# Moving a token tile's preparation steps in the v stage of an attention kernel

## The chip, the cores and the metric

The kernel runs on one core of one Trainium2 chip. The metric is device time in microseconds (us) of one launch, median over several runs. All numbers are float32; the large matrix products are made from operands that are split into a high part and a low part, with three passes (high x high, high x low, low x high).

## The reference, cut to what matters

The reference normalises `x` (4 x 512 tokens of 512 features), runs a lightning attention with 16 heads of width 128 over it, and multiplies its output with a gate from a router (softmax over 64 experts, top 8). The part that this case is about is the first one, the normalised tokens and the product that gives `v`:

```python
xn = _layernorm(x, axis=-1)                                   # x: 4 x 512 x 512
qkv = silu(einsum('bnf,of->bno', xn, w_qkv))                   # v is a third of it
...
logits = einsum('th,eh->te', xn, router_weight) + router_bias  # from the same tokens
```

The attention proper, the norm over all heads, the output product and the gate follow. They are not touched.

## The kernel before, in words

TensorE makes nearly every product, and each of the other engines works through its own list in the order in which the program issues it. No scheduler reorders anything: the order is written out by hand. VectorE (DVE in the profile) does the adds out of PSUM and part of the splits, ScalarE (ACT) the copies, the casts to the high part and the SiLU, GpSimd (POOL) most of the low parts, SyncE (SP) the transfers.

**Token tiles.** The 2048 tokens are handled as eight tiles `(p, t)`: `p` is a pair of sequences (two of four), `t` a block of 128 tokens in each. A tile is prepared in these steps (`prepare`, line 849): `stats` (BN statistics on VectorE, and a power on GpSimd that gives `rstd`), `norms` (two normalisations on VectorE), `turn` (eight transposes on TensorE, two copies by ScalarE into `xf`), `sums` (four subtractions of 128x256 into `ts`, which give T1 to T4), `plain` (high and low parts of B11, B21 and B22) and `more` (high and low parts of T1 to T4). A high part is a cast on ScalarE (line 100), a low part a subtraction (line 103) on the engine named.

**Units of v.** The loop at line 957 runs over sixteen units `k`: unit `k` multiplies one tile with one of two groups of v's weights, the first eight units with group 0. Units 0 and 1 use plain block products (`plain_unit`, line 554), the others a Strassen form with seven products (`unit`, line 515), 6 matmuls each. In a Strassen unit three PSUM banks are used several times:

- product one writes bank 0, and ScalarE copies it to `s1`; product four accumulates onto bank 0, so it waits for that copy;
- product two writes bank 1, and VectorE adds `a` = bank 1 + `s1`; product five starts bank 1 again and waits for `a`;
- product three writes bank 2, and VectorE adds `e` = bank 2 + `a`; product six accumulates onto bank 2 and waits for `e`;
- after product five VectorE adds bank 1 and `e` into the output `vo11`; product seven accumulates onto bank 1 and waits for that add. The outputs `vo01` and `vo10` come after products six and seven.

**The list `after`.** While unit `k` runs, the steps of later tiles are issued between its products. `after[i]` holds what is issued behind product i + 1; `after[0]` is behind product one. The transposes of tile k + 1 stand behind product one. The engines' queues follow that order: an instruction that stands in front of an add on VectorE delays it. The weights need the same treatment: `sum_of` (line 452) makes four weight sums on VectorE, 128x1024 each, behind product four in units 3 to 6 for group 1; `split_one` (line 475) splits a weight block. `split_rw` (line 310) splits the router's weights once, in time for `logits` in unit 8.

**Outputs.** `vout` is the pool for the outputs of a unit, 128x512 each (`sink`, line 598), and for three temporaries of `logits`. A place in it is free again when its store has landed.

The functions that the change touches and what calls them:

Of the kernel before, what the change touches and what calls it, by code (L numbers as in the profile page):

```python
# [50 lines left out]
def kernel(  # L51
# [13 lines left out]
    nc = tc.nc  # L65
# [5 lines left out]
    NT = N // P  # L71
# [6 lines left out]
    def pool(stack, name, bufs=1, **kw):  # L78
        return stack.enter_context(tc.tile_pool(name=name, bufs=bufs, **kw))


    def left(stack, name, bufs=1):
        return pool(stack, name, bufs, side="left", reuse_waits="tile")
# [15 lines left out]
    def split_hi(hi, src):  # L99
        nc.scalar.copy(hi, src)  # L100

    def split_lo(eng, lo, src, hi):
        eng.tensor_tensor(lo, src, hi.bitcast(F32), ALU.subtract)  # L103
# [74 lines left out]
    stats = [const.tile([P, NT, 2], F32, tag=f"stats{b}", name=f"stats{b}") for b in range(B)]  # L178
# [59 lines left out]
    def normalise_x(p, t):  # L238
        for b in range(p * PB, p * PB + PB):
            normalise(xts[b, t], xts[b, t], b, t)  # L240

    xfs = {}


    def transpose(stage, p, j, t, copy=True):
        b = p * PB + j
        if j == 0:
            xfs[p, t] = stage.tile([P, PB, FC, P], F32, tag="xf", name=f"xf_{p}_{t}", bufs=2)
        pt = ps_sc.tile([P, FC, P], F32, tag="sc", name=f"pt_{b}_{t}")
        for c in range(FC):  # L250
            nc.tensor.transpose(pt[:, c, :], xts[b, t][:, bass.ts(c, P)], ident)  # L251
        if copy:
            nc.scalar.copy(xfs[p, t][:, j], pt)
        return pt

    def halves(xf):
        return xf[:, 0, 0:KC], xf[:, 1, 0:KC], xf[:, 0, KC:], xf[:, 1, KC:]

    def split_blocks(p, t, eng, srcs):
        for n, src in srcs:  # L260
            blk = blocks[p, n][:, t]
            split_hi(blk[:, 0], src)
            split_lo(eng, blk[:, 1], src, blk[:, 0])


    def token_sums(eng, xf, s):
        b11, b12, b21, b22 = halves(xf)
        sub = lambda d, a, b: lambda: eng.tensor_tensor(d, a, b, ALU.subtract)
        subs = [
            sub(s[:, 0], b12, b11), sub(s[:, 1], b22, s[:, 0]),  # L270
            sub(s[:, 2], b22, b12), sub(s[:, 3], b21, s[:, 1]),
        ]
        return subs, {
            "B11": b11, "B21": b21, "B22": b22, "T1": s[:, 0], "T2": s[:, 1], "T3": s[:, 2], "T4": s[:, 3],
        }


    def combine(stage, p, t, eng, again=""):
        src = {}

        def sums():
            s = stage.tile([P, 4, KC, P], F32, tag="ts", name=f"ts_{p}_{t}{again}", bufs=1)
            subs, of = token_sums(eng, xfs[p, t], s)
            src.update(of)
            for f in subs:
                f()

        def split(which):
            split_blocks(p, t, eng, [(n, src[n]) for n in XN if n[0] == which])
        return sums, lambda: split("B"), lambda: split("T")  # L290


    def plain(p, t, eng):
        b11, b12, b21, b22 = halves(xfs[p, t])
        split_blocks(p, t, eng, (("B11", b11), ("T1", b12), ("B21", b21), ("B22", b22)))
# [14 lines left out]
    def split_rw(stage):  # L310
        rwr.append(stage.tile([P, FC, 2, E], F32R, tag="rwr", name="rwr", bufs=1))
        split_hi(rwr[0][:, :, 0], rw)
        split_lo(nc.vector, rwr[0][:, :, 1], rw, rwr[0][:, :, 0])
# [533 lines left out]
    NP_FIRST = 2  # L847

    def prepare(stage, p, t):
        first = (p, t) == (0, 0)  # L850

        def turn():
            for j in range(PB):
                transpose(stage, p, j, t)
            if p == 0:
                nc.sync.dma_start(out=xf_d[t], in_=xfs[p, t])

        if p == 0 and t < NP_FIRST:
            sums = (lambda: plain(p, t, nc.vector if t == 0 else nc.gpsimd)), lambda: None, lambda: None
        else:  # L860
            sums = combine(stage, p, t, nc.gpsimd)

        return {
            "stats": lambda: layer_norms(p, t, first), "norms": lambda: normalise_x(p, t),
            "turn": turn, "sums": sums[0], "plain": sums[1], "more": sums[2],
        }
# [33 lines left out]
    vw_stack, vs_stack = ExitStack(), ExitStack()  # L900
    stage = right(vs_stack, "stage", 4)
    rawp, sump = right(vs_stack, "vraw"), right(vs_stack, "vsum")
    vwp, vout = left(vw_stack, "vw", 8), left(vw_stack, "vout", 4)
    ws = [v_weights(0, g, rawp, sump, vwp) for g in range(NV)]
    tiles = [(p, t) for p in range(NP) for t in range(NT)]
    again = [(p, t) for p in reversed(range(NP)) for t in range(NT)]
    n1 = len(tiles)
    prep = [prepare(stage, p, t) for p, t in tiles]

    load_pair(stage, 0, 0)  # L910
# [46 lines left out]
    for k, (p, t) in enumerate(tiles + again):  # L957
        g, after = k // n1, nothing()
        if n1 - NT <= k < n1:
            after[6].append(lambda p=p, t=t: keep_blocks(p, t))  # L960
        if k + 1 < n1:
            after[0 if k else 1].append(prep[k + 1]["turn"])
            if 0 < k < n1 - 3:
                after[0].append(lambda k=k: load_pair(stage, *tiles[k + 3]))
            if k == 0:
                after[1].insert(0, prep[2]["stats"])
            after[1].append(prep[k + 1]["sums"])
            if k + 2 < n1:
                if k:
                    after[1].append(prep[k + 2]["stats"])  # L970
                after[4 if k > 1 else 3].append(prep[k + 2]["norms"])
            after[1].append(prep[k + 1]["plain"])
            after[4].append(prep[k + 1]["more"])
        if k == 0:
            after[0].append(lambda: warm_up(8, xfs[0, 0][:, 1, 0]))
        if k == n1 - 1:
            after[2].append(lambda: split_rw(stage))
        for unit_of, p2 in ((n1, 1), (n1 + NT + 1, 0)):
            if k == unit_of:
                less = [lambda p2=p2, what=what: scores_less(p2, what) for what in ("top", "less")]  # L980
                for j, f in enumerate(logits(stage, p2, vout) + less):
                    after[j].append(f)
        if k < NP_FIRST:
            for i in range(2):
                n, eng = f"S{2 * k + i + 1}", nc.gpsimd if i else nc.vector
                after[2 * i + 2].append(lambda i=2 * k + i: ws[0].sum_of(i, nc.vector))
                after[2 * i + 3].append(lambda n=n, eng=eng: ws[0].split_one(n, eng))
        if k == NP_FIRST:
            after[0].append(ws[1].load())
        if n1 - 5 <= k < n1 - 1:  # L990
            after[3].append(lambda n=k - n1 + 5: ws[1].sum_of(n, nc.vector))
        for n, unit_of, step, eng, piece in (
            ("A11", n1 - 2, 6, nc.gpsimd, None), ("S2", n1 - 1, 0, nc.gpsimd, None),
            ("S1", n1 - 1, 1, nc.gpsimd, None), ("A12", n1 - 1, 2, nc.vector, 0),
            ("S3", n1 - 1, 3, nc.gpsimd, None), ("A12", n1 - 1, 4, nc.vector, 1),
            ("S4", n1, 1, nc.vector, 0), ("S4", n1, 2, nc.vector, 1), ("A22", n1, 0, nc.gpsimd, None),
        ):
            if k == unit_of:
                after[step].append(lambda n=n, eng=eng, piece=piece: ws[1].split_one(n, eng, piece))
        if n1 <= k < n1 + NT:  # L1000
            after[0].append(lambda t=t: load_xf(stage, t))
        if n1 < k <= n1 + NT:
            sums, split_plain, split_sums = combine(stage, 0, k - n1 - 1, nc.gpsimd, "r")
            after[1] += [sums, split_plain]
            after[4].append(split_sums)
        if k == NP_FIRST:
            after[0].append(keep_rows)
        if k >= n1:
            for i in range(2):
                after[3 * i + 2].append(lambda h=2 * (k - n1) + i: keep_decay(h))  # L1010
        if k == n1 + NT + 2:
            after[0].append(scores_exp)
        if k == 2 * n1 - 2:
            vs_stack.close()
            todo = [(p, *u) for p in range(NP) for u in h_units(p, hw_stack)]
            todo[0][3].load()()
            todo[1][3].load()()
        if k == 2 * n1 - 1:
            weight_steps(todo[0][3], after)
        v_unit(p, g, t, ws[g], vout, after, k < NP_FIRST)  # L1020
# [29 lines left out]
    again = right(rb_stack, "again")  # L1050
# [5 lines left out]
    for i, (p, kind, n, w) in enumerate(todo):  # L1056
        after = nothing()
# [161 lines left out]
```

## Time and profile before

| | us |
|---|---|
| median of 3 runs | 1064.3 |
| lowest and highest | 1062.9, 1064.8 |
| profiled execution, its own time | 1063.0 |
| span of the profiled execution | 1061.2 |
| TensorE busy in it | 1050.7 |
| VectorE, ScalarE, GpSimd busy | 524.3, 521.8, 663.7 |

TensorE's clock was granted in full (0.999). The first 189 us of the span are the v stage; units 0 to 7, in which the tiles are prepared, lie between 11 and 103 us. From 40 to 100 us GpSimd is busy 57.5 of 60 us and VectorE 41.5. A line of the timeline gives start, duration, engine, line, operation, output and inputs, shapes and count, and in brackets the idle time of the engine before it and what ended it. A line of waits gives who waited for whom, the total, how often, and the longest.

### The profile page before, as it was taken

To read this page: it belongs to the slowest core of one execution; us is meant where nothing else is said; L and a number is where in the kernel's file an instruction comes from. 1 tells how busy PE (TensorE), PEld (TensorE's weight loads), DVE (VectorE), ACT (ScalarE), POOL (GpSimd) and SP (SyncE) were. 2 spreads that over 40 slices of the span, in tenths; PEclk is the share of its full clock that TensorE was granted. 3 is DMA by queue.
4 is the path that set the end of the run, shared out by engine and by line. 5 is a ranking of instruction groups with operands and counts; after the bars stand their busy time and mean duration, and the time that the engine had idled before them with its cause. 6 is when DMAs were issued, how large, how long until landed. Compare 5 with 4: busy or idle time off the path is not lost.

```text
span 1061.2 us, 16043 instructions
## 1 busy us (share of the span) xinstructions
PE 1050.7 (99%) x5707; PEld 906.1 (85%) x5707; DVE 524.3 (49%) x872; ACT 521.8 (49%) x960; POOL 663.7 (63%) x694
## 2 busy tenths in 40 slices
PE   9899999999999999999999999999999999999998
PEld 7687888888888888888888888888888888888886
DVE  6676434355454545444444444444444456745354
ACT  5556454655555555455555555554555543332221
POOL 5899571757777678677785777767867756402020
PEclk9999999999999999999999999999999999999999
DMA  7467655422423223334822242232322446455351
GB/s 243 163 231 285 225 172 171 154 86 85 140 85 95 78 94 117 96 124 156 290 91 65 85 129 86 85 102 90 107 66 85 157 132 217 136 162 171 99 189 50
DMA packets 109871, 143.07 MB, mean 135 GB/s; under 512 B 9680, under 2 KB 58208, under 8 KB 108896
## 3 DMA queue, kind: packets, MB, share of 16 engines
q1 hardware_dynamic: 108752, 141.35, 41.3%
q8 instruction: 45, 0.74, 0.3%
q10 hardware_dynamic: 1040, 0.71, 0.2%
q14 instruction: 34, 0.28, 0.1%
HBM read 93.24 MB, written 50.87 MB: 136 GB/s over the span
## 4 chain that ended last, share of the span: by engine, by line
PE 95%; DVE 0%; issue 0%
PE u_qk L533 29%; PE po L838 16%; PE u_g L533 14%; PE u_v L533 12%; PE o L726 5%; PE sa L689 5%; PE o L728 4%; PE ss L712 4%; PE kt L692 2%; PE pu L783 1%; PE lg L324 1%; PE pt L251 0%; PE ssq L755 0%; PE lt L350 0%; PE pw L419 0%
## 5 line engine op out<-in xcount | busy, mean ns | idle before, releaser
L838 PE MATMUL po<-wr,yr 128*128 128x512 f32 (+1 forms) x777 | 178.7, 388 | 0.9 <-DVE u L825 0.9
L838 PEld LDWEIGHTS po<-wr,yr 128*128 128x128 f32 x777 | 144.4, 188 | 30.4 <-DVE u L825 1.1
L533 PE MATMUL u_qk<-blk_T,ws_qk 128*128 128x512 f32 x576 | 147.0, 395 | 0.0
L738 POOL TENSOR_TENSOR sqs<-sqs,sq 128x512 f32<-128x512 f32 x60 | 77.9, 1298 | 76.3 <-ACT sq L737 76.3
L533 PEld LDWEIGHTS u_qk<-blk_T,ws_qk 128*128 128x128 f32 x576 | 105.8, 188 | 20.2
L103 POOL TENSOR_TENSOR ws_qk<-sum_qk,ws_qk 128x512 fp32r<-128x512 f32 x64 | 82.8, 1294 | 40.5 <-ACT ws_qk L100 39.6
L533 PE MATMUL u_qk<-blk_B,wa_qk 128*128 128x512 f32 x384 | 99.1, 394 | 0.0
L726 PE MATMUL o<-at,vin 128*128 128x128 f32 x512 | 88.5, 275 | 0.0
L533 PEld LDWEIGHTS u_qk<-blk_B,wa_qk 128*128 128x128 f32 x384 | 71.0, 188 | 14.1
L103 DVE TENSOR_TENSOR yr<-yin,yr 128x512 fp32r<-128x512 f32 x64 | 60.6, 960 | 43.0 <-ACT yr L100 42.1
L103 POOL TENSOR_TENSOR ws_g<-sum_g,ws_g 128x512 fp32r<-128x512 f32 x32 | 41.3, 1289 | 59.9 <-ACT ws_g L100 59.9
L726 PEld LDWEIGHTS o<-at,vin 128*128 128x128 f32 x512 | 74.9, 192 | 2.5
L533 PE MATMUL u_g<-blk_T,ws_g 128*128 128x512 f32 x288 | 76.0, 400 | 0.0
L698 ACT ACTIVATE kd<-kt,kdecay 128x384 f32<-128x384 f32 x64 | 37.2, 582 | 78.0 <-PE kt L692 78.0
L730 DVE SCALAR_TENSOR_TENSOR y<-o,nw,gt 128x512 f32<-128x512 f32 x64 | 48.1, 751 | 55.1 <-PE o L728 55.1
L728 PE MATMUL o<-qd,st 128*128 128x128 f32 x384 | 74.3, 275 | 0.0
L737 ACT ACTIVATE sq<-o 128x512 f32<-128x512 f32 x60 | 35.9, 598 | 75.2 <-POOL sqs L738 42.4
L716 DVE SCALAR_TENSOR_TENSOR st<-st,bdecay,ss 128x128 f32<-128x128 f32 x128 | 41.7, 346 | 58.9 <-ACT st L714 56.6
L826 POOL TENSOR_TENSOR u<-u,x 128x512 f32<-128x512 f32 x12 | 17.8, 1515 | 84.0 <-DVE u L825 84.0
L100 ACT CAST yr<-yin 128x512 fp32r<-128x512 f32 x64 | 39.2, 616 | 63.2 <-PE po L838 39.2
L577 ACT ACTIVATE k<-k 128x512 f32<-128x512 f32 x64 | 40.4, 632 | 57.1 <-DVE k L524 57.1
L689 PE MATMUL sa<-q,k 128*128 128x128 f32 x512 | 67.5, 275 | 0.0
(192 smaller groups left out, 2296.1 us busy)
## 6 DMA issues: line engine op xcount, KB each, us to landing
v<-vo_v SPq DMA_DIRECT2D x64, 256.0 KB, 2.2
raw_qk<-in_w_head_dram SPq DMA_DIRECT2D x64, 256.0 KB, 3.8
vin<-v SPq DMA_DIRECT2D x64, 256.0 KB, 3.6
y<-y SPq DMA_DIRECT2D x64, 256.0 KB, 2.0
yin<-y SPq DMA_DIRECT2D x64, 256.0 KB, 2.8
x<-in_x_dram SPq DMA_DIRECT2D x32, 256.0 KB, 4.6
raw_g<-in_w_head_dram SPq DMA_DIRECT2D x32, 256.0 KB, 3.0
raw_v<-in_w_v_dram SPq DMA_DIRECT2D x16, 256.0 KB, 6.1
```

The costliest lines, as they stand in the source:

```text
L100: nc.scalar.copy(hi, src)
L103: eng.tensor_tensor(lo, src, hi.bitcast(F32), ALU.subtract)
L533: nc.tensor.matmul(ps, lhsT, rhs, start=(first and c == 0 and n == 0), stop=(c == KC - 1 and n == len(PASSES) - 1), skip_group_check=not f ...
L577: nc.scalar.activation(dst, src, AF.Silu)
L689: nc.tensor.matmul(pa[:, c], k[:, c], q[:, c], start=True, stop=True)
L712: nc.tensor.matmul(ps[:, c], kd[s][:, c], v_of(b, h, c), start=True, stop=True)
L716: nc.vector.scalar_tensor_tensor(r[:, c], r[:, c - 1], bdecay[:, h : h + 1], ps[:, c], ALU.mult, ALU.add)
L726: nc.tensor.matmul(o, v_of(b, h, c), at[s][:, c], start=True, stop=(c == 0))
L728: nc.tensor.matmul(o, st[s][:, c - 1], qd[s][:, c - 1], start=False, stop=True)
L730: nc.vector.scalar_tensor_tensor(y, po, nw[:, h : h + 1], gts[s], ALU.mult, ALU.mult)
L738: nc.gpsimd.tensor_tensor(sq[b], sq[b], s1, ALU.add)
L838: nc.tensor.matmul(pos[t][:, c], yr[:, yi, bass.ts(t, P)], wos[h][:, wi, c], start=(h == 0 and n == 0), stop=(h in stops and n == len(PASS ...
```

## The change

Six things are moved or resized, and no arithmetic changes.

- The four token sums of tile k + 1 go from GpSimd to VectorE. Where they stand among the products stays: behind product two. Tiles 0 and 1 have none, and the second preparation of pair 0 (units 9 to 12) keeps them on GpSimd.
- The statistics of tile k + 2 stand behind product one, in front of the add `a`, no longer behind product two, between `a` and `e`. On GpSimd their power stands in front of the low parts of B and no longer behind the sums.
- The high and low parts of T1 to T4 (`more`) stand behind product four in the Strassen units, no longer behind product five. In units 0 and 1 they stay.
- For units 0 and 1 the rest of the order is kept, except that in unit 1 the statistics come in front of the sums.
- The split of the router's weights goes from behind product three of unit 7 to behind product seven of unit 4.
- `vout` has six places in the place of four.

```diff
-    def combine(stage, p, t, eng, again=""):
+    def combine(stage, p, t, sum_eng, eng, again=""):
         src = {}
 
         def sums():
             s = stage.tile([P, 4, KC, P], F32, tag="ts", name=f"ts_{p}_{t}{again}", bufs=1)
-            subs, of = token_sums(eng, xfs[p, t], s)
+            subs, of = token_sums(sum_eng, xfs[p, t], s)
...
-            sums = combine(stage, p, t, nc.gpsimd)
+            sums = combine(stage, p, t, nc.vector, nc.gpsimd)
...
-    vwp, vout = left(vw_stack, "vw", 8), left(vw_stack, "vout", 4)
+    vwp, vout = left(vw_stack, "vw", 8), left(vw_stack, "vout", 6)
...
             after[0 if k else 1].append(prep[k + 1]["turn"])
             if 0 < k < n1 - 3:
                 after[0].append(lambda k=k: load_pair(stage, *tiles[k + 3]))
-            if k == 0:
-                after[1].insert(0, prep[2]["stats"])
-            after[1].append(prep[k + 1]["sums"])
+
             if k + 2 < n1:
-                if k:
-                    after[1].append(prep[k + 2]["stats"])
+                after[0 if k else 1].append(prep[k + 2]["stats"])
+                if k == 0:
+                    after[1].reverse()
                 after[4 if k > 1 else 3].append(prep[k + 2]["norms"])
-            after[1].append(prep[k + 1]["plain"])
-            after[4].append(prep[k + 1]["more"])
+            after[1] += [prep[k + 1]["sums"], prep[k + 1]["plain"]]
+            after[4 if k < NP_FIRST else 3].append(prep[k + 1]["more"])
         if k == 0:
             after[0].append(lambda: warm_up(8, xfs[0, 0][:, 1, 0]))
-        if k == n1 - 1:
-            after[2].append(lambda: split_rw(stage))
+        if k == NT:
+            after[6].append(lambda: split_rw(stage))
...
-            sums, split_plain, split_sums = combine(stage, 0, k - n1 - 1, nc.gpsimd, "r")
+            sums, split_plain, split_sums = combine(stage, 0, k - n1 - 1, nc.gpsimd, nc.gpsimd, "r")
```

## The prediction

> **What bounds the kernel now.** I read the page first: TensorE is busy 1050.7 of 1061.2 us and the chain that ended last is 95% TensorE. So any gain must come out of TensorE's waits, and any loss must make new ones. I then asked for the waits of TensorE alone, the whole of them:
>
> ```profile
> PE warm L150 <- POOL ident masks.py:199: 1.4, 1, 1.4
> PE u_v L533 <- POOL blk_B L103: 1.4, 1, 1.4
> PE u_v L533 <- ACT s_v L539: 1.0, 1, 1.0
> PE po L838 <- DVE u L825: 0.9, 1, 0.9
> PE u_v L533 <- DVE vo_v L524: 0.7, 1, 0.7
> PE u_v L533 <- POOL blk_T L103: 0.3, 1, 0.3
> PE u_v L533 <- DVE e_v L524: 0.3, 1, 0.3
> ```
>
> Five of these are in v (the u_v rows): 1.4 + 1.0 + 0.7 + 0.3 + 0.3 = 3.7 us. That is the most this change can gain. Third, the timeline says where they are, with the work that released them:
>
> ```profile
> 37.02 1.81 DVE L202 TENSOR_SCALAR x<-x,stats,rstd 128x512 f32<-128x512 f32 x2 [4.76 <-POOL rstd L236]
> 37.73 1.44 PE L533 MATMUL u_v<-w_A_v,blk_B 128*128 128x512 f32 x5 [1.38 <-POOL blk_B L103]
> 40.62 2.79 PE L533 MATMUL u_v<-w_S_v,blk_T 128*128 128x512 f32 x11 [0.34 <-POOL blk_T L103]
> 41.04 1.76 DVE L469 TENSOR_TENSOR sum_v<-raw_v,sum_v 128x1024 f32<-128x1024 f32 x1
> 42.83 1.05 ACT L100 CAST w_S_v<-sum_v 128x1024 fp32r<-128x1024 f32 x1 [5.07 <-DVE sum_v L469]
> 44.41 1.66 PE L533 MATMUL u_v<-w_A_v,blk_B 128*128 128x512 f32 x6 [1.00 <-ACT s_v L539]
> 47.75 0.74 PE L533 MATMUL u_v<-w_S_v,blk_B 128*128 128x512 f32 x2 [0.32 <-DVE e_v L524]
> 98.23 1.45 DVE L103 TENSOR_TENSOR rwr<-rw,rwr 128x256 fp32r<-128x256 f32 x1 [0.24 <-ACT rwr L100]
> 102.03 1.66 PE L533 MATMUL u_v<-w_A_v,blk_T 128*128 128x512 f32 x6 [0.70 <-DVE vo_v L524]
> ```
>
> To be seen: four waits lie in unit 2, the first Strassen unit (36 to 48 us), and one in unit 7 (102 us), behind the split of the router weights. In unit 2 GpSimd is late. It makes the four token sums before rstd and before the low part of B11, so VectorE idles 4.76 us for rstd, and everything behind that (S3's low part, sum3, S4's cast on ScalarE, the copy s1 behind it) is late too.
>
> In the other units TensorE does not wait, but by little. This is unit 5, the rows that decide most below:
>
> ```profile
> 72.09 1.53 PE L533 MATMUL u_v<-w_A_v,blk_B 128*128 128x512 f32 x6
> 75.99 0.69 DVE L524 TENSOR_TENSOR a_v<-u_v,s_v 128x512 f32<-128x512 f32 x1 [2.39 <-PE u_v L533]
> 79.21 1.22 DVE L469 TENSOR_TENSOR sum_v<-raw_v 128x1024 f32<-128x1024 f32 x1
> 80.34 0.69 DVE L524 TENSOR_TENSOR vo_v<-u_v,e_v 128x512 f32<-128x512 f32 x1
> 81.16 1.57 PE L533 MATMUL u_v<-w_A_v,blk_T 128*128 128x512 f32 x6
> ```
>
> The add into vo11 ends at 81.03 and product seven, which accumulates onto the bank it reads, starts at 81.16. In unit 2 and unit 7 a product started 0.05 us after such an add ended (102.03 after 101.98). So vo11 has some 0.1 us to spare in a unit that has a weight sum (units 3 to 6).
>
> **The price of a sum on VectorE.** The trace has no token sum on VectorE. The nearest row alone is the low parts of the first tile, same shape, two SBUF inputs: 0.76 us for two. The dearest is the router split above, 1.45 us for 256 elements, behind a GpSimd subtraction of 128x512. Between them lies a train of VectorE instructions beside a train of GpSimd ones:
>
> ```profile
> 12.41 0.76 DVE L103 TENSOR_TENSOR blk_B<-xf,blk_B 128x256 fp32r<-128x256 f32 x2
> 17.16 1.00 DVE L202 TENSOR_SCALAR x<-x,stats,rstd 128x512 f32<-128x512 f32 x2 [0.82 <-POOL rstd L236]
> 36.94 2.48 POOL L103 TENSOR_TENSOR blk_B<-xf,blk_B 128x256 fp32r<-128x256 f32 x3
> ```
>
> The two normalisations take 1.00 alone at 17.16 and 1.81 at 37.02, beside these three low parts, which themselves stretch from 0.7 to 0.9 each. The two engines take turns, one instruction each, about 0.9 a turn. Adds with a PSUM source (a, e, vo) and BN statistics stay at 0.69 in both surroundings. So four sums cost 1.5 us alone, 3.6 in strict turns, 5.8 by the dearest row; I take turns only against those GpSimd instructions that are ready at that time.
>
> Here a rule speaks for the change. The Trainium skill, "GPSIMD Engine Reference", section 4.1 Engine selection, sends elementwise work to VectorE, since GpSimd is about twice as slow for two inputs. The rows alone agree (0.38 against 0.74), and by that rule the sums cost 1.5 us and no unit gets a new wait. The row that bears on it is the turn of 0.9, and "SBUF — State Buffer" (The single rule) is behind it: the port pair of the two engines is an exclusive lock, and issue order decides who blocks. By the rule the result is a gain of some 2.2 us, by the row a small loss. I follow the row, because GpSimd has its B low parts ready just when the sums come.
>
> **The change part by part** (products counted from one; the instruction order of the built kernel shows TensorE's order unchanged, 24 sums moved from GpSimd to VectorE).
>
> *Unit 2.* VectorE: the statistics of tile 3 still end at 30.74. The sums of tile 2 then alternate with S2's low part on GpSimd (29.89 to 33.42): first at 31.1 to 31.5, the second only after GpSimd's second half at about 32.6, the last at 33.6 to 34.3. Then sum2 (1.2 plus a turn) to 35.3, the normalisations (1.8) to 37.1, S3's low parts (2.3) to 39.4, sum3 (1.7) to 41.05. On ScalarE S4's cast ends at 42.1 and s1 at 42.6. GpSimd now has rstd at 33.3 and B11's low part at 34.1 to 34.8: the waits of 1.38 and 0.34 go. TensorE ends product three at 40.9 and waits for s1 until 42.65, against 44.41 before. So 1.76 gained there, though a wait of 1.7 remains: what is late next is S4's cast in front of s1.
> After it the new order costs. The statistics of tile 4 (2.0 us) now stand in front of a: 41.0 to 43.0, a to 43.65. The sums of tile 3 issue at 43.6, where GpSimd has just begun the second half of S4's low part (1.3 us), so the first sum waits to 44.6; e ends at 46.3 to 47.0. Product six, due at 45.4, starts at 46.35 to 47.05, against 47.75: a gain of 0.7 to 1.4. If the chain up to S4's cast is 0.7 later (all its turns lost) the gain is 0. I take 0.75.
>
> *Units 3 to 6*, offsets from the unit's first matmul (72.09 in the rows above). The previous vo10 ends at 0.9, statistics to 2.85, rstd on GpSimd to 3.55; a at 3.9 to 4.6 as before. B low parts on GpSimd from 3.55. ScalarE has both copies by 3.2. Sums: the first waits for B11's end (4.3) or B21's (4.9), the second takes its turn after B22's start; last sum ends at 7.0 (2.4 us for four). e ends at 7.6; product six is due at 7.71: no wait, but no room. Before, e ended at 79.30, offset 7.2. The weight sum (1.1 us of lock) therefore issues at 7.5, not 7.1. Just then the T low parts, moved from behind product five to behind product four, become ready: ScalarE does vo00 to 7.15 and T2's cast to 7.46. If VectorE gets in first, the sum ends at 8.7, vo11 at 9.33, product seven starts at 9.38 instead of 9.07: 0.3. If GpSimd does, 0.6 later: 0.9. In before GpSimd got in first at 70.5, issued 0.04 us after VectorE. I take 0.6 for units 3, 4 and 6: 1.8 us lost. From both sides: 0 if the sums find GpSimd idle, 0.9 each otherwise.
>
> *Unit 5 with the router split.* It now stands behind product seven of unit 4: ScalarE 0.41 in front of s1, VectorE 0.45 once that cast is there (offset 2.0 to 2.4), in front of the statistics. Statistics end at 4.3, a at 4.95, the sums at 8.0, e at 8.6: product six waits 0.9, and the weight sum and vo11 come after it, 0.3 to 0.9 more. I take 1.5 in all.
>
> *Unit 7.* Without the split A12's cast is 0.3 earlier and its low part goes at 99.3, vo11 at 99.9 to 100.6, before product seven is due at 101.3: 0.70 gained.
>
> *At no cost.* Six output places: they remove a wait of ScalarE (58.35, for the store of vo) and one of VectorE (91.86); neither reached TensorE, and the stores stay in the same order on SP. Statistics one step earlier need x loaded: SP issues those loads a unit ahead (56.18 for statistics at 66.1), and they land in 4.6 (page); of 10 us of cover 5 are left, and the statistics move up by 3. The second load of tile 0 (SP) now waits on VectorE's sums instead of GpSimd's, long done in unit 8. T casts pass vo11's SiLU on ScalarE: 1.3 us later, and the place of vo11 is not written again for six tiles, a unit and a half (15 us). GpSimd loses 4 x 0.74 = 3.0 us a unit; it is not awaited in units 3 to 7, so that is worth nothing by itself. From unit 8 on the order is the same.
>
> *Sum.* Gains 0.75 + 0.70 = 1.45; losses 1.8 + 1.5 = 3.3; net 1.85 us slower. Against the profiled execution (1063.0, span 1061.2) that is a span of 1063.0. That execution lies 1.3 below the median of 1064.3; the difference is carried over: 1066.1.
>
> **The rivals.**
> *Slower, GpSimd first in every unit.* Place: the weight sum against T2's low part at offset 7.5. Price: 0.9 in units 3, 4 and 6 (2.7), 1.85 in unit 5, and nothing gained in unit 2: 4.55 - 0.7 = 3.85, so 1068.1. It decides from the point where the last sum ends after offset 6.9. For it: the sample at 70.5. Against it: in unit 3 vo10 ends earlier, and GpSimd's B low parts come earlier against the sums.
> *Faster, sums slip in between.* If the four sums take near 1.5 us, units 3 to 6 wait nowhere and unit 2 keeps 1.4 or more: 2.1 to 3.7 less, about 1061.8. For it: GpSimd is left 3.0 us freer in each unit. Against it: the idle time is not where the sums are.
> *It evens out.* VectorE gets in first everywhere: 0.3 in units 3, 4 and 6 (0.9) and 0.3 to 1.2 in unit 5, against the 1.45 gained: -0.25 to +0.65, so 1064.05 to 1064.95.
>
> **How the numbers follow.** A measurement of this kernel can tell about 0.2% from no change, 2.1 us, so the bounds are 1062.2 and 1066.4. My own forecast 0.45, most of it (0.36) inside the bound, 0.09 over it; the slower rival 0.33; evening out 0.12; faster 0.10. Same 0.48, slower 0.42, faster 0.10. The likeliest case alone spans 1064.5 to 1067.5; the range runs from the near end of the faster rival to just past the slower one, 1062.1 to 1068.8.
>
> **What would show it.** Right: TensorE's waits for POOL blk_B and blk_T gone from unit 2, one for ACT s_v of 1 to 2 us left, and one for DVE e_v; new waits of 0.3 to 0.9 for DVE vo_v in units 3 to 6, the largest in unit 5; none at unit 7; the sums' rows on VectorE at a mean of 0.5 to 0.7. Wrong: sums at 0.4 with no u_v waits after 50 us (faster), or TensorE waiting for GpSimd, a stretch that I hold free.

## The result, and the profile after

The changed kernel takes 1064.75 us in the median against 1062.6 for the kernel before: 2.15 us more, a ratio of 1.0021 with an interval of 1.0014 to 1.0028. Each median is over 20 runs; one run of the kernel before took 2040.5 us, the other 19 lie between 1061.9 and 1064.8. The profiled execution has a span of 1062.9 against 1061.2 us. First the busy times on the page of the changed kernel:

```profile
PE 1051.0 (99%) x5707; PEld 905.1 (85%) x5707; DVE 539.0 (51%) x896; ACT 522.6 (49%) x960; POOL 649.9 (61%) x670
```

VectorE gained 14.7 us and GpSimd lost 13.8, less than the 24 sums that moved: they take 17.5 us on VectorE (0.73 each) and would have been 17.8 at GpSimd's 0.74. On GpSimd most of the difference is in the low parts of T, whose mean rose from 828 to 1041 ns; on VectorE the router split fell from 1.45 to 0.42 us. TensorE's busy time is all but unchanged, so what counts lies in its waits, here those in v (who waited for whom: total us, times, longest):

```profile
PE u_v L533 <- DVE e_v L524: 3.1, 3, 1.6
PE u_v L533 <- ACT s_v L539: 1.5, 1, 1.5
...
PE u_v L533 <- DVE vo_v L524: 0.9, 2, 0.6
```

The two waits for GpSimd are gone. In their place stand longer ones for VectorE. TensorE's timeline of the changed kernel says where (start, duration, engine, line, what; in brackets the idle time and what ended it):

```profile
41.84 1.67 PE L533 MATMUL u_v<-w_A_v,blk_B 128*128 128x512 f32 x6 [1.46 <-ACT s_v L539]
46.51 1.66 PE L533 MATMUL u_v<-w_S_v,blk_B 128*128 128x512 f32 x6 [1.62 <-DVE e_v L524]
...
68.20 1.66 PE L533 MATMUL u_v<-w_S_v,blk_B 128*128 128x512 f32 x6 [0.17 <-DVE e_v L524]
70.15 1.66 PE L533 MATMUL u_v<-w_A_v,blk_T 128*128 128x512 f32 x6 [0.29 <-DVE vo_v L524]
...
80.80 1.67 PE L533 MATMUL u_v<-w_S_v,blk_B 128*128 128x512 f32 x6 [1.28 <-DVE e_v L524]
...
94.11 1.66 PE L533 MATMUL u_v<-w_A_v,blk_T 128*128 128x512 f32 x6 [0.59 <-DVE vo_v L524]
```

The first two lie in unit 2, the next two in unit 4, then one each in units 5 and 6. Unit 7, where TensorE waited 0.70 us before, has none. (In this line form a group that follows without a wait takes 1.52, one after a wait 1.66.)

The listed idle time is not the whole price of a wait, so from here on I use the length of a unit: the start of its product one to the start of the next unit's, read off TensorE's timeline. A column gives the start of unit 2, and one the lowest run, for a reason that follows.

| kernel | unit 2 | 3 | 4 | 5 | 6 | 7 | sum 2 to 7 | unit 2 starts | median | lowest |
|---|---|---|---|---|---|---|---|---|---|---|
| before | 14.69 | 10.99 | 10.46 | 10.48 | 10.44 | 10.51 | 67.57 | 35.95 | 1062.6 | 1061.9 |
| after | 14.15 | 10.79 | 11.48 | 12.40 | 11.56 | 9.52 | 69.91 | 35.22 | 1064.75 | 1064.2 |
| a1 | 20.16 | 12.15 | 11.93 | 11.94 | 11.07 | 10.51 | 77.76 | 37.04 | 1073.4 | 1073.1 |
| a2 | 14.04 | 11.47 | 10.41 | 10.43 | 10.44 | 9.52 | 66.31 | 35.14 | 1061.0 | 1060.3 |
| a3 | 14.19 | 10.44 | 10.41 | 10.77 | 10.44 | 9.52 | 65.77 | 34.94 | 1060.0 | 1059.9 |
| a4 | 14.23 | 10.78 | 11.48 | 11.56 | 11.58 | 10.54 | 70.16 | 35.01 | 1064.6 | 1064.3 |
| b1 | 11.78 | 10.79 | 10.80 | 12.07 | 10.72 | 9.54 | 65.70 | 38.61 | 1064.1 | 1062.1 |
| b2 | 14.17 | 10.94 | 11.47 | 12.39 | 11.58 | 9.55 | 70.10 | 35.07 | 1065.1 | 1063.9 |
| b3 | 12.83 | 10.41 | 10.43 | 10.44 | 10.41 | 9.52 | 64.04 | 37.12 | 1059.6 | 1058.2 |
| b4 | 12.81 | 10.41 | 10.43 | 10.44 | 10.41 | 9.52 | 64.02 | 35.19 | 1059.1 | 1058.4 |
| c1 | 10.48 | 12.44 | 10.43 | 10.44 | 10.41 | 9.52 | 63.72 | 37.42 | 1060.2 | 1058.1 |
| c2 | 14.52 | 11.03 | 10.46 | 10.48 | 10.44 | 9.52 | 66.45 | 38.32 | 1061.5 | 1060.9 |

A unit without a wait takes 10.41 us (unit 7, which has no transposes, 9.52). The span is the start of unit 2, plus the sum, plus 957.5 to 958.0 in every kernel; so nothing outside the start-up and units 2 to 7 changed by more than 0.5 us. The start of unit 2 moves by up to 3.7 us between the traces, and the runs of one kernel fall into groups about 2 us apart (b3: 1058.2 to 1058.7, 1060.4 to 1060.7 and one at 1062.5). That the groups come from the start-up is likely but not shown, as only one execution of each kernel has a trace. Medians carry that scatter. The sums do not, except that a late start can shorten unit 2: by 2.4 us in b1 against after, though c2, which starts as late, is only 0.2 shorter there than before. The lowest runs stand to each other as the sums do, within 0.7 us for all but a1 and b1. So: after lost 2.34 us in units 2 to 7, of which units 4, 5 and 6 lost 1.02 + 1.92 + 1.12, and units 2, 3 and 7 gained 0.54 + 0.20 + 0.99.

### The profile page after: what moved, and what is told of

Read it like the earlier page. It is cut to its first block, busy times and chain, and to the rows that moved or that the text cites. A ratio compares the mean times of both kernels' runs of the same rounds, so it can differ in the third digit from the quotient of the medians.

```text
span 1062.9 us, 16055 instructions
## 1 busy us (share of the span) xinstructions
PE 1051.0 (99%) x5707; PEld 905.1 (85%) x5707; DVE 539.0 (51%) x896; ACT 522.6 (49%) x960; POOL 649.9 (61%) x670
## 4 chain that ended last, share of the span: by engine, by line
PE 91%; DVE 1%; issue 0%; ACT 0%; DMA 0%; POOL 0%; POOLq 0%
PE u_qk L533 29%; PE po L838 16%; PE u_g L533 14%; PE u_v L533 8%; PE sa L689 5%; PE o L726 5%; PE o L728 4%; PE ss L712 4%; PE kt L692 2%; PE pu L783 1%; PE lg L324 1%; PE ssq L755 0%; DVE vo_v L524 0%; DMA bd_T<-blk_T 0%; PE pw L419 0%
## 5 line engine op out<-in xcount | busy, mean ns | idle before, releaser
L826 POOL TENSOR_TENSOR u<-u,x 128x512 f32<-128x512 f32 x12 | 17.8, 1517 | 83.9 <-DVE u L825 83.9
```

## The experiments

*Theory.* The sums stand in front of e on VectorE and take turns with GpSimd's B low parts; that makes e, the weight sum and vo11 late. In units 4 and 6 T2's low part, which comes a product earlier now, takes another turn in front of vo11. *Rival.* The move of the statistics, or the router split behind product seven of unit 4, makes the loss, and the engine of the sums matters little. The first four experiments separate these.

**a1: before, with the sums on VectorE and nothing else.** (The new parameter of `combine` is that of the change.)

```diff
-            sums = combine(stage, p, t, nc.gpsimd)
+            sums = combine(stage, p, t, nc.vector, nc.gpsimd)
```

> Edit: the kernel before, with the four token sums of each tile on VectorE and nothing else changed; the statistics stay between the sums and the add e. Theory (VectorE's place in front of e is what counts): sums (1.6 us here, since GpSimd waits for rstd behind the statistics) and statistics (2.0) both stand in front of e, so e ends some 8.9 us after the unit's start where 7.7 is due, and the weight sum then meets GpSimd's B low parts. Units 3 to 6 are each 1.5 to 2.2 us longer, units 3 to 7 some 6 to 8 in all, the run 1067 to 1070 against 1062.6. Rival (moving the statistics or the other edits made the loss, the sums by VectorE are free or a gain since GpSimd is relieved): units 3 to 6 stay at 10.5, the run at 1061 to 1063.

Measured: 1073.4 us against 1062.6, a ratio of 1.0098 (1.0084 to 1.0111). The direction is right, the place mostly not. Units 3 to 5 lost 1.16 to 1.47 and unit 6, which has no statistics, 0.63. In units 3 to 5 the sums meet no GpSimd work at all and take 0.42 each: GpSimd's power waits for the statistics behind them, and its B low parts for the power. It is enough that sums (1.5 us) and statistics (2.0) both stand between a and e. So it seems to be the move of the statistics in front of a that makes room for sums on VectorE at all: a3 below has the same sums of 0.42, the statistics in front of a, and no such wait in units 3, 4 and 6. No run moves the statistics alone.

Half the loss (5.47 of 10.19) is in unit 2, where no expectation had one. TensorE's timeline and, below it, the windows around that wait (length, busy time of PE, PEld, DVE, ACT and POOL, then the granted clock, the DMA share and GB/s):

```profile
51.91 2.93 PE L533 MATMUL u_v<-w_S_v,blk_B 128*128 128x512 f32 x6 [3.22 <-DVE e_v L524]
54.64 2.76 PE L533 MATMUL u_v<-w_A_v,blk_T 128*128 128x512 f32 x6
```

```profile
48.00:50.00 2.00, 0.69 (x4) 0.22 (x2) 1.93 (x6) 0.02 (x1) 0.00 (x0) 1.00 0.98 302
50.00:52.00 2.00, 0.09 (x1) 0.09 (x1) 1.80 (x7) 0.00 (x0) 0.66 (x2) 0.70 0.82 285
52.00:54.00 2.00, 2.00 (x5) 1.62 (x6) 1.97 (x3) 1.33 (x4) 2.00 (x4) 0.50 0.98 325
54.00:56.00 2.00, 2.00 (x6) 1.52 (x6) 0.69 (x1) 0.92 (x3) 2.00 (x4) 0.50 1.11 361
...
58.00:60.00 2.00, 2.00 (x15) 1.74 (x14) 0.13 (x1) 1.65 (x4) 0.00 (x0) 1.00 0.75 281
```

The first sum takes 1.41 us behind S4's low part on GpSimd (from 46.70), the other sums and the statistics follow, and TensorE waits 3.22 us for e. Within that idle time, at 50.8 us, the granted clock falls to 0.50, and it is back only at 57.6 (read off windows of 0.2 us). Products six and seven take 2.73 and 2.56 us from start to start where 1.36 is usual: 2.6 us lost on top of the wait. "TensorE: Matmul & The Clock Gate" of the Trainium skill (HAM oscillation) warns of idle gaps above about 3.4 us, its closing table of gaps above about 3; 3.22 were enough here. After's 1.62 us at 46.51 and the 2.51 us of a2 below, before 38.04, were not (granted clock 1.00 throughout), nor were the shorter waits earlier in this unit, which before has too.

**a2: after, with the sums back on GpSimd.**

```diff
-            sums = combine(stage, p, t, nc.vector, nc.gpsimd)
+            sums = combine(stage, p, t, nc.gpsimd, nc.gpsimd)
```

> Edit: the changed kernel, with the token sums back on GpSimd and everything else of the change kept. Theory: nothing stands between a and e on VectorE, so the waits for e and vo11 in units 3 to 6 go (10.4 to 10.6 us each, from 10.8, 11.5, 12.4, 11.6), also in unit 5 in spite of the router split; unit 7 stays at 9.5; unit 2 keeps part of its gain, because rstd now stands ahead of the sums on GpSimd (13 to 14 us, from 14.2). Units 2 to 7 some 65 to 66.5 us against 69.9 and 67.6 before; the run 1060 to 1061.5, below the kernel before. Rival (the order of the statistics and the router split make the loss): units 4 to 6 keep 11.4 or more, the run at 1064 to 1065.

Measured: 1061.0 us, ratio to before 0.9981 (0.9975 to 0.9988). Units 4, 5 and 6 are at 10.41 to 10.44 again, although the statistics and the router split stay where the change put them. The rival falls. Against before it gains 0.65 in unit 2 and 0.99 in unit 7 and loses 0.48 in unit 3. What is left is GpSimd being late at the start of units 2 and 3:

```profile
PE u_v L533 <- POOL blk_B L103: 3.2, 2, 2.5
...
PE u_v L533 <- POOL blk_T L103: 0.5, 1, 0.5
```

**a3: after, with the B parts of units 2 to 6 behind product four, so that GpSimd is idle while the sums run.**

```diff
-            after[1] += [prep[k + 1]["sums"], prep[k + 1]["plain"]]
+            after[1].append(prep[k + 1]["sums"])
+            after[1 if k < NP_FIRST else 3].append(prep[k + 1]["plain"])
```

> Edit: the changed kernel, with the high and low parts of B (plain) issued behind product four, ahead of those of T, in the Strassen units. The sums stay on VectorE in their place; GpSimd has nothing to do while they run. Theory (taking turns with the B low parts is what makes the sums long): the sums fall from a mean of some 0.75 us to 0.42, e is in time, the weight sum issues before the B low parts are ready; units 3, 4 and 6 at 10.4 to 10.6 us, unit 5 at 10.4 to 11, units 2 to 7 some 65.5 to 67.5 us, the run 1060.5 to 1062.5. Rival (VectorE simply has too much work in front of e, with or without GpSimd): units 4 to 6 remain at 11.4 to 12.4, the run 1064 to 1065.

Measured: 1060.0 us, ratio 0.9971 (0.9960 to 0.9982). The sums stay on VectorE, and units 3, 4 and 6 are without a wait all the same. Unit 5 of after, VectorE and GpSimd:

```profile
76.50 0.69 DVE L524 TENSOR_TENSOR a_v<-u_v,s_v 128x512 f32<-128x512 f32 x1
77.10 0.42 DVE L268 TENSOR_TENSOR ts<-xf 128x256 f32<-128x256 f32 x1
77.31 2.56 POOL L103 TENSOR_TENSOR blk_B<-xf,blk_B 128x256 fp32r<-128x256 f32 x3
77.56 0.84 DVE L268 TENSOR_TENSOR ts<-xf,ts 128x256 f32<-128x256 f32 x1
78.32 0.96 DVE L268 TENSOR_TENSOR ts<-xf 128x256 f32<-128x256 f32 x1
79.20 0.95 DVE L268 TENSOR_TENSOR ts<-xf,ts 128x256 f32<-128x256 f32 x1
80.07 0.68 DVE L524 TENSOR_TENSOR e_v<-u_v,a_v 128x512 f32<-128x512 f32 x1
```

and the same unit of a3:

```profile
74.72 0.69 DVE L524 TENSOR_TENSOR a_v<-u_v,s_v 128x512 f32<-128x512 f32 x1
75.33 0.41 DVE L268 TENSOR_TENSOR ts<-xf 128x256 f32<-128x256 f32 x1
75.77 0.42 DVE L268 TENSOR_TENSOR ts<-xf,ts 128x256 f32<-128x256 f32 x1
76.11 0.42 DVE L268 TENSOR_TENSOR ts<-xf 128x256 f32<-128x256 f32 x1
76.45 0.42 DVE L268 TENSOR_TENSOR ts<-xf,ts 128x256 f32<-128x256 f32 x1
76.79 0.68 DVE L524 TENSOR_TENSOR e_v<-u_v,a_v 128x512 f32<-128x512 f32 x1
77.55 3.24 POOL L103 TENSOR_TENSOR blk_B<-xf,blk_B 128x256 fp32r<-128x256 f32 x3 [1.98 <-ACT blk_B L100]
```

From the end of a to the start of e it is 2.88 us in after (77.19 to 80.07) and 1.38 in a3 (75.41 to 76.79). The same four instructions cost twice as much when GpSimd's three B low parts run between them. That is the theory's main step, shown by a2 (other engine) and a3 (same engine, other time). Unit 2 keeps its waits for s1 and e (1.5 and 1.6).

**a4: after, with the router split back in unit 7.**

```diff
-        if k == NT:
-            after[6].append(lambda: split_rw(stage))
+        if k == n1 - 1:
+            after[2].append(lambda: split_rw(stage))
```

> Edit: the changed kernel, with the split of the router's weights back behind product three of unit 7. Theory: unit 5 falls from 12.4 to 11.4 us, as the other units that have all the steps; unit 7 rises from 9.5 to 10.5; the two cancel and the run stays at 1064.5 to 1065. Rival (unit 5 is long for another reason): unit 5 stays at 12.4 and the run rises to 1065.7.

Measured: 1064.6 us, ratio 1.0022 (1.0014 to 1.0029). The split moves a loss from unit 7 to unit 5: unit 5 falls by 0.84, unit 7 rises by 1.02, and the wait of before is back there:

```profile
103.66 1.67 PE L533 MATMUL u_v<-w_A_v,blk_T 128*128 128x512 f32 x6 [0.68 <-DVE vo_v L524]
```

This wait also shows what a wait costs. In a4's timeline product six of that unit starts at 101.46, product seven 2.20 later instead of 1.36, the next unit 1.51 after that instead of 1.36: 0.84 + 0.15 = 0.99 for a listed 0.68.

**b1: after, with the T parts back behind product five. b2: after, with four output places.**

```diff
-            after[4 if k < NP_FIRST else 3].append(prep[k + 1]["more"])
+            after[4].append(prep[k + 1]["more"])
```

> Edit: the changed kernel, with the high and low parts of T (more) back behind product five in the Strassen units. Theory: in units 4 to 6 the weight sum no longer finds GpSimd in T2's low part and issues first, so it takes 1.2 us instead of 1.4 to 1.7 and vo11 is earlier; the wait for vo11 in units 4 and 6 (0.3 and 0.6) goes, the wait for e stays (0.2 to 1.3). Units 4 and 6 some 0.3 to 0.6 us shorter each (11.48 to about 11.0, 11.56 to about 11.0), units 2 to 7 69.0 to 69.5 us, the run 1063.7 to 1064.5. Rival (the T parts are not what holds the weight sum up): units 4 and 6 as in the changed kernel, the run 1064.7.

Measured: 1064.1 us, ratio 1.0007 (0.9999 to 1.0015). The median alone decides nothing: the runs lie at 1062.1 to 1062.8 and from 1063.6 on, and the profiled one, at 1063.6, reached unit 2 only at 38.61 us. The units decide: 4 and 6 fall by 0.68 and 0.84, unit 5 by 0.33, and unit 3 does not move. (The lowest run fits: it is 2.1 us below after's, where units 3 to 7 give 1.8.) All four weight sums take 1.21 us here. So of what units 4 and 6 lost in after, the early T parts made 0.68 and 0.84, and the sums by themselves the rest, 0.34 and 0.28. After shows why unit 3 is the exception. Units 3, 4 and 6 of after, VectorE and GpSimd around the weight sum (sum_v):

```profile
56.80 1.21 DVE L469 TENSOR_TENSOR sum_v<-raw_v 128x1024 f32<-128x1024 f32 x1
56.87 2.44 POOL L103 TENSOR_TENSOR blk_T<-ts,blk_T 128x256 fp32r<-128x256 f32 x2 [1.54 <-ACT blk_T L100]
...
67.68 3.98 POOL L103 TENSOR_TENSOR blk_T<-ts,blk_T 128x256 fp32r<-128x256 f32 x4 [0.75 <-ACT blk_T L100]
68.06 1.43 DVE L469 TENSOR_TENSOR sum_v<-sum_v,raw_v 128x1024 f32<-128x1024 f32 x1
...
91.64 3.10 POOL L103 TENSOR_TENSOR blk_T<-ts,blk_T 128x256 fp32r<-128x256 f32 x3 [1.05 <-ACT blk_T L100]
91.73 1.72 DVE L469 TENSOR_TENSOR sum_v<-raw_v,sum_v 128x1024 f32<-128x1024 f32 x1
```

In unit 3 VectorE started 0.07 us before GpSimd and kept its 1.21 us. In unit 6 it started 0.09 after, and the sum took 1.72. a4 and b2 repeat both: 0.10 us ahead in unit 3 (a4) the sum took 1.21, 0.04 behind in unit 6 of a4 and in unit 4 of b2 it took 1.77.

```diff
-    vwp, vout = left(vw_stack, "vw", 8), left(vw_stack, "vout", 6)
+    vwp, vout = left(vw_stack, "vw", 8), left(vw_stack, "vout", 4)
```

> Edit: the changed kernel, with four output places again. Theory: at no cost, as the prediction had it; units within 0.1 us of the changed kernel's, the run 1064.3 to 1065. Rival (a place that comes late holds vo00 on ScalarE, and T's casts behind it): a unit or two longer by 0.3 or more, the run 1065 to 1066.

Measured: 1065.1 us, ratio 1.0021 (1.0014 to 1.0027), and the units of after within 0.15 us. The places make no difference that shows.

**b3: a3, with the router split behind product seven of unit 6, and in unit 2 the sums behind e.**

```diff
-            after[1].append(prep[k + 1]["sums"])
+            after[2 if k == NP_FIRST else 1].append(prep[k + 1]["sums"])
...
-        if k == NT:
+        if k == n1 - 2:
```

> Edit: the changed kernel with B's parts behind product four (as a3_b_later), and two more: in unit 2 alone the token sums stand behind e (behind product three), and the router split stands behind product seven of unit 6, where VectorE has neither statistics nor normalisations. Theory: unit 2 loses its wait for e (1.6), for vo11 some 0.3 remains, so 14.2 falls to 12.4 to 12.9; unit 5 falls from 10.8 to 10.4; unit 7 stays at 9.5. Units 2 to 7 some 63.6 to 64.2 us against 65.8 of a3_b_later and 67.6 before; the run 1058 to 1058.6. Rival (the sums behind e only shift the wait to product seven or to unit 3): unit 2 and 3 together stay at 24.6, the run at 1059.7.

Measured: a sum of 64.04 us, 3.5 below before, in the interval that was expected; units 3 to 7 have no wait left. The median of 1059.6 (ratio 0.9967, 0.9955 to 0.9979) is higher than expected because half of the runs lie in the later groups (1060.4 and above); the other half, 1058.2 to 1058.7, is about where it was expected. What is left in unit 2:

```profile
PE u_v L533 <- ACT s_v L539: 1.5, 1, 1.5
...
PE u_v L533 <- DVE vo_v L524: 0.3, 1, 0.3
```

**b4: b3, with S4's cast on ScalarE and its low part on GpSimd moved from in front of s1 to behind it.**

```diff
-                after[2 * i + 3].append(lambda n=n, eng=eng: ws[0].split_one(n, eng))
+                if n != "S4":
+                    after[2 * i + 3].append(lambda n=n, eng=eng: ws[0].split_one(n, eng))
+        if k == NP_FIRST:
+            after[0].insert(1, lambda: ws[0].split_one("S4", nc.gpsimd))
```

> Edit: b3_unit2_rw6 with the split of S4 moved from the end of unit 1 to unit 2, behind product one, so that ScalarE copies s1 ahead of S4's cast. Theory: the wait of product four for s1 (1.5) goes; product five then waits for a, which stands behind the statistics (42.9 against 43.3 of the changed kernel), so only 0.4 to 1.0 of the 1.5 is gained; unit 2 at 11.8 to 12.3 us, the run 1057.3 to 1058.2. Rival (S4's cast ahead of vo00 and the B casts delays tile 3): unit 3 longer by what unit 2 gains, the run as b3_unit2_rw6.

Measured: 1059.1 us, ratio 0.9966 (0.9955 to 0.9978); unit 2 is 12.81 us long, not shorter than in b3. The expectation is missed. (b3's trace starts unit 2 1.9 us later, but the lowest runs, 1058.4 against b3's 1058.2, show no gain either.) The wait for s1 went, as meant, and came back behind a and vo11:

```profile
PE u_v L533 <- DVE a_v L524: 1.2, 1, 1.2
...
PE u_v L533 <- DVE vo_v L524: 0.6, 1, 0.6
```

S4's cast was only the last of a late train. VectorE itself, with the statistics in front of a, is as late as s1 was.

**c1: b4, with unit 2's list on VectorE reordered.** The statistics stand behind e, the sums behind vo11, then the normalisations; the T parts follow the sums. The split stands behind product seven of unit 6 as in b3. The edit also has lines in `combine` that name B's blocks ahead of the sums, and the lines of b4; they are not shown here.

```diff
-                after[0 if k else 1].append(prep[k + 2]["stats"])
+                after[2 if k == NP_FIRST else 0 if k else 1].append(prep[k + 2]["stats"])
...
+            two = k == NP_FIRST
+            after[4 if two else 1].append(prep[k + 1]["sums"])
+            after[4 if k <= NP_FIRST else 3].append(prep[k + 1]["more"])
+            if two:
+                after[4].append(prep[k + 2]["norms"])
```

> Edit: b4_s4_later with another order in unit 2 alone: on VectorE a, e, the statistics of tile 4, vo11, and only then the token sums and the normalisations; T's parts behind the sums. Theory (b4 only moved the wait from s1 to a, because the statistics stood in front of it): product five no longer waits for a, vo11 waits 0.3 to 0.6 us for the statistics, the transposes of unit 3 some 0.5 for the normalisations; units 2 and 3 together 21.3 to 22.2 us against 23.2, the run 1057 to 1058.2. Rival (the preparation of tiles 3 and 4 is the limit, so what unit 2 gains unit 3 loses): units 2 and 3 together 23 or more, the run 1059 or more.

Measured: 1060.2 us, ratio 0.9966 (0.9954 to 0.9979). Unit 2 is almost without a wait at 10.48, but unit 3 takes 12.44, because its transposes now wait for the normalisations behind those sums:

```profile
50.46 0.63 PE L251 MATMUL pt<-ident,x 128*128 128x128 f32 x4 [1.03 <-DVE x L202]
51.33 0.63 PE L251 MATMUL pt<-ident,x 128*128 128x128 f32 x4 [0.24 <-DVE x L202]
```

Units 2 and 3 together are 22.92 against 23.22 in b4, still 2.1 us above two free units (20.82): most of the waiting only changed its place. That misses the expectation (21.3 to 22.2) and is just under the rival's 23. Whether the start of the pipeline can be made shorter than that was not tried further.

**c2: before, with the router split behind product seven of unit 6 and nothing else.** The edit is one to the line `if k == n1 - 1` of before, which becomes `n1 - 2`, and to `after[2]` below it, which becomes `after[6]`.

> Edit: the kernel before, with the split of the router's weights behind product seven of unit 6 and nothing else. Theory: unit 7 falls from 10.5 to 9.5 us, no other unit moves by more than 0.1; units 2 to 7 66.6 us against 67.6, the run 1061.5 to 1061.9 against 1062.6. Rival (A12's split, which stands behind the router's, is what product seven of unit 7 waits for): unit 7 stays at 10.2 to 10.5, the run at 1062.5.

Measured: 1061.5 us, ratio 0.9987 (0.9980 to 0.9993). Unit 7 falls from 10.51 to 9.52, units 4 to 6 stay. The split, which runs at the start of unit 7, costs nothing there: that unit has no transposes, statistics or weight sum that it would delay.

Faster than before by about 0.3% are a3, b3, b4 and c1, whose intervals overlap; by the sums of the units the last three are 3.5 to 3.9 us shorter than before, a3 1.8.

## Why the prediction was right, and where its terms were not

The forecast was slower by 1.85 us, at 1066.1. It is slower by 2.15; the time of 1064.75 is lower than forecast because the 20 runs of before have their median at 1062.6, not at the 1064.3 of three runs from which the prediction started. (So 1064.75 also lies in the range given for "it evens out", but that rival allowed a loss of 0.65 at most.) That the span, 1062.9, is within 0.1 of the forecast is luck in part: after's trace starts unit 2 0.73 us earlier than before's, and units 2 to 7 lost 2.34. The main step, that the sums alternate with GpSimd's B low parts and that e, the weight sum and vo11 come late for it, is what a2, a3 and b1 show. Term by term:

- **Unit 2, a gain of 0.75 forecast, 0.54 measured.** Right in its places: the waits for blk_B and blk_T are gone, the wait for s1 is 1.46 (1.7 forecast), and e follows with 1.62. That S4's cast is what held s1 up was only part of it: b4 took the cast away and gained nothing. Nor is the gain owed to the sums: a2, with the sums on GpSimd and the rest as in after, has 14.04 there, with other waits.
- **Units 3, 4 and 6, a loss of 0.6 each forecast; measured a gain of 0.20 and losses of 1.02 and 1.12.** The 0.6 was a mean over two outcomes, and the trace has both, each near its price. VectorE was first in unit 3: 0.38 above a free unit, where 0.3 was forecast. GpSimd was first in units 4 and 6: 1.02 and 1.12, where 0.9 was forecast; without the early T parts b1 leaves 0.34 and 0.28 of it, the forecast's 0.3. In unit 4 e itself also came 0.17 late, where "no wait, but no room" was forecast. The step that failed is the choice of a mean, and in unit 3 the base: the prediction took that unit for free of waits before, though it was 0.58 above a free one, so that 0.38 is a gain. The slower rival's mechanism held in two of the three units.
- **Unit 5, a loss of 1.5 forecast, 1.92 measured.** Right: the split's cast, its low part, the statistics, a, the sums and e follow each other without a gap, and product six waits 1.28 (0.9 forecast). The split's share is 0.84 by a4; the rest, 1.08, is as much as units 4 and 6 pay. One sign did not come: the wait for vo11 was to be largest here, but this unit's listed wait is for e alone, and those for vo11 are in units 4 and 6 (0.29 and 0.59).
- **Unit 7, a gain of 0.70 forecast, 0.99 measured.** The term was read from the listed idle time. The same error lies under the statement that 3.7 us is the most that this change can gain. Before stood 6.0 us above six free units (67.57 against 5 x 10.41 + 9.52 = 61.57), and c1 gained 3.85.
- **The price of a sum, 0.9 in turns, 0.5 to 0.7 in the mean forecast.** Measured over all 24 in after (ns: lowest, median, highest):

```profile
L268 DVE TENSOR_TENSOR ts<-xf x12: 410/718/1333, 30.0 to 89.9; 128x256 f32<-128x256 f32 x12
L268 DVE TENSOR_TENSOR ts<-xf,ts x12: 411/845/1399, 30.7 to 90.8; 128x256 f32<-128x256 f32 x12
```

  Their mean is 728 ns, just above the range. In b3, where most find GpSimd idle, it is 500. By the rule of the Trainium skill, "GPSIMD Engine Reference" (4.1 Engine selection), the prediction had an estimate of 1.5 us for four; a3's unit 5 has about that (1.38 from a to e). In after the row of the turn decided. "SBUF — State Buffer" (The single rule) calls the port pair of the two engines an exclusive lock and lets issue order decide who blocks; units 3 and 6 of after, a4 and b2 agree (0.04 to 0.10 us ahead or behind). The row at 70.5 of before, which the prediction names, does not: VectorE's normalisation starts 0.04 us ahead there, and it took 1.07 us while GpSimd's low part at 70.50 took its usual 0.74. So starts this close do not always tell, and that a port is what the two share is the page's account, not shown by a run here.
- **No cost for six places:** right, by b2.

The sum came out only 0.3 to 0.5 us off by luck, because the errors partly cancel: units 4, 5 and 6 cost 1.4 more than forecast and unit 2 gave 0.2 less, while unit 3 cost 0.8 less and unit 7 gave 0.3 more.

The move of the sums by itself is worth little even when it is done well: a3 against a2, the same order with the sums on the one or the other engine (and the B parts moved), is 65.77 against 66.31. The larger gains of the good versions are the router split in a unit that has room (1.0, c2) and, in unit 2, sums behind e (1.4, b3 against a3; the wait for e, 1.6, is gone, and the lowest runs are 1.7 apart, of which unit 5 makes 0.3).

## What to carry to other kernels

Price an instruction with two SBUF inputs on VectorE by what GpSimd has ready at the same moment, not by its own row: four 128x256 sums cost 1.4 us with GpSimd idle and 2.9 beside three of its low parts, and putting those parts later was worth a little more (4.1 us, a3 against after) than choosing the other engine (3.6, a2). Work that is issued only once belongs in the unit that lacks the steps which it would delay. When the run times scatter by 2 us, compare stage lengths from the trace and the lowest runs with each other before believing a median.

## What the runs showed of the hardware that was not expected

- A TensorE idle time of 3.22 us brought its granted clock down to 0.50 2.1 us after it began, for 6.8 us (50.8 to 57.6 in a1), and cost another 2.6 us in the two products after it. Waits of 2.51 us (a2) and 1.62 us (after) did not.
- A wait cost TensorE about 0.3 us more than its listed idle time (a4, unit 7): 0.16 up to the start of the waiting group, and 0.15 in that group. At 46.51 of after it was 0.33 by the same reckoning.
- The start of unit 2 varies from 34.9 to 38.6 us, with waits of TensorE for the low parts of A21 (b3) and for the normalised tokens (b1, c2) in the start-up. Why these are late in some executions is open.
